# The end of a two-layer kernel: one matmul unit moved, the last gate tile by tile, the last store in halves by two queues

## The chip, the cores and the metric

The kernel runs on one core of one Trainium2 chip. The metric is the device time of one execution in microseconds (us). The profile is that of one execution; times inside it are counted from the start of its span. TensorE (PE) does the matrix products, VectorE (DVE) and ScalarE (ACT) the elementwise work, GpSimd (POOL) very little, and SyncE (SP) issues nearly all DMA transfers.

## The reference

The input `x` has 4 batches of 512 rows with 256 columns, in float32. Two layers follow each other. Each normalizes `x` over its columns, computes a mixing branch `s` and a feed-forward branch, and adds their gated product. The second layer, whose end is concerned here, cut to what matters:

```python
xn = layernorm(x)
s = causal_attention(xn)               # with its own layernorm, out-projection and residual
up_gate = einsum('bsd,hd->bsh', xn, W1)
up_lin  = einsum('bsd,hd->bsh', xn, W3)
hidden  = fwht(silu(up_gate) * up_lin) # Walsh-Hadamard transform over 1024 columns
ffn     = einsum('bsh,dh->bsd', hidden, W2)
x = x + s * silu(ffn)                  # the gate
return x
```

## The kernel before, in words

The rows of a batch form four tiles of 128 rows each (t = 0 to 3), and a tile's rows lie on the 128 partitions. The kernel walks through the four batches of the first layer and then through the four of the second, with the attention of a batch and the preparation of the next placed between the matrix products of the feed-forward part. The transform is folded into the weights `w2`. Products are done with split operands: each float32 operand is kept as a high part (rounded by ScalarE, L61) and a low part (the rest, subtracted by VectorE, L62), and three matmuls take the place of one: high by high, high by low, low by high.

`ffn_s` (L560) is the feed-forward part of one batch of the second layer. It makes the hidden values in four groups (q = 0 to 3), each of two blocks of 128 hidden columns (c = 0, 1). The down projection of tile t is a sum over all eight pairs (q, c). The inner function `down` (L577) issues it in units: one unit is one (q, c) for one tile, three matmuls of 128x256 into that tile's PSUM buffer, `f_3dn` in the profile. In the last batch each tile has a PSUM buffer of its own.

In the last batch (`last` is set) most units run between the up products, as the list `places` says. What is left is written out as a list of (q, c, t) at the end of `ffn_s`, L681 to L684. The very last group, q = 3, makes its second half of hidden values (tiles 2 and 3) in two pieces, c = 0 and c = 1 (L666 to L669): a Silu on ScalarE, a multiply on VectorE, the rounding on ScalarE, the subtraction on VectorE. The order of the matmuls is fixed as the code writes it (`line["fixed"]`, L66 to L72). On the other engines a scheduler sets the order, unless `after(...)` (L462) puts an instruction behind another; `after` fixes the order alone.

After the unit (3, 1) of a tile, which finishes its sum, `last` is called. It is `gate_tile` (L1055), which for tile t

- applies Silu to the tile's PSUM buffer on ScalarE and writes `gl` (L1058),
- multiplies `gl` by the attention branch `s` on VectorE (L1059),
- adds the product to `x` on VectorE (L1060); it reads what the multiply wrote, and waits for it on a semaphore,
- stores the tile's 128 rows of 1 KB by one DMA issued on SP (L1061).

On VectorE the scheduler had arranged the eight gate operations of the last batch in this order: multiply 0, multiply 1, add 0, add 1, multiply 2, multiply 3, add 2, add 3. The four stores stand on SP in the order of the tiles. Each DMA signals one of eight semaphores, which are taken in turn ("lanes" in this text); before a lane is used again, the issuing engine checks that its earlier transfer has landed. After the last store SP waits for all eight lanes in five wait instructions, two semaphores at most in each, and then the closing barriers of all engines follow.

ScalarE issues only two DMAs in the kernel before: loads of two tiles of `x` at the very start (L104). They run in a queue of their own, q10; SP's run in q1.

Of the kernel before, what the change touches and what calls it, by code (L numbers as in the profile page):

```python
# [17 lines left out]
ALU = mybir.AluOpType  # L18
# [3 lines left out]
P = 128  # L22
D = 256
B = 4
# [3 lines left out]
NT = S // P  # L28
# [7 lines left out]
def kernel(ctx: ExitStack, tc: tile.TileContext, a: dict, out: bass.AP):  # L36
    nc = tc.nc
# [9 lines left out]
    def t2(name, shape, dt=F32):  # L47
        return act.tile(shape, dt, tag="t2", name=name, bufs=6)
# [171 lines left out]
    def sl(i):  # L220
        return slice(i * P, (i + 1) * P)
# [240 lines left out]
    def after(ins):  # L462
        return tc.issue_after(ins.ins) if ins else nullcontext()
# [96 lines left out]
    def ffn_s(name, b, pairs, w2, beside, before, last=None):  # L560
# [16 lines left out]
        def down(q, c, hs, tiles):  # L577
            for t in tiles:
                hh, hl = (h[:, c, sl(t % 2)] for h in hs[t // 2])
                o = out_of(t)  # L580
                for n, (l, r) in enumerate(((hh, w2h), (hh, w2l), (hl, w2h))):
                    matmul(
                        o, l, r[:, 2 * q + c, :],
                        start=q + c + n == 0 and (t % 2 == 0 or last is not None),
                        stop=q == NH // 2 - 1 and c == 1 and n == 2,
                        skip_group_check=True,
                    )
# [92 lines left out]
            return behind, dns  # L680
        for q, c, t in (  # L681
            (2, 0, 2), (2, 1, 2), (2, 0, 3), (2, 1, 3), (3, 0, 0), (3, 1, 0), (3, 0, 1), (3, 1, 1),
            (3, 0, 2), (3, 0, 3), (3, 1, 2), (3, 1, 3),
        ):  # L684
            down(q, c, hidden[q], (t,))
            if (q, c) == (3, 1):
                last(t, outs[t])
# [222 lines left out]
    def run(f, *args):  # L910
        return lambda: f(*args)
# [34 lines left out]
    first = {"table": None}  # L946
# [108 lines left out]
    def gate_tile(t, o):  # L1055
        x, s = xs[B - 1][:, t, :], xns[1, B - 1][:, t, :]
        g = t2(f"gl{t}", [P, D])
        nc.scalar.activation(g, o, AF.Silu)  # L1058
        nc.vector.tensor_tensor(g, g, s, ALU.mult)  # L1059
        nc.vector.tensor_tensor(x, x, g, ALU.add)  # L1060
        nc.sync.dma_start(out[B - 1, sl(t), :], x)  # L1061

    loaded = {}

# [12 lines left out]
    for b in range(B):  # L1077
# [15 lines left out]
        if not final:  # L1093
# [3 lines left out]
            rows = run(next, norms[b + 1])  # L1097
# [14 lines left out]
            if b + 2 < B:  # L1112
                norms[b + 2] = norm(1, b + 2)
                places[3][7].append(run(next, norms[b + 2]))
            behind, dn = ffn_s(f"f1_{b}", b, pairs(b), w2_1, places, behind)
        else:
            later = [[(q, c, (2, 3)) for c in range(2)] for q in range(2)]
# [3 lines left out]
                [[later[1][0]], [later[1][1]], [], [0], [], [1], [], []],  # L1121
            ]
            ffn_s(f"f1_{b}", b, pairs(b), w2_1, places, behind, last=gate_tile)


# [66 lines left out]
```

## Time and profile before

| what | us |
|---|---|
| median of 3 runs | 359.26 (359.16 to 359.29) |
| the profiled execution | 359.27 |
| its span | 357.5 (357.49) |
| what lies around the span | 1.78 |
| busy: PE, DVE, ACT | 351.5, 287.1, 197.6 |

The profiled execution agrees with the median within 0.01 us, so its span can stand for the runs. TensorE is busy for 98% of the span, and the clock granted to it was full all the time. The time after TensorE's last matmul is short: the page puts the last matmul's end at about 353.2, and the rest of the span, some 4.3 us, is gate, stores and closing.

In the profile a line such as `351.80 0.42 DVE L1059 ...` has the start and the length in us, the engine, the source line, the operation, and `out<-in` by buffer names. An entry with `x2` merges two neighbours; its length then is from the start of the first to the end of the second. `SPq` is the instruction queue of SP, whose DMA issues are shown with the time that the issue itself takes, not the transfer.

### The profile page before, as it was taken

The numbers are of one execution on the slowest core, as the hardware profiler recorded it, in microseconds if no ns is written. First come the engines' busy times: TensorE is split into PE (matmuls) and PEld (weight loads), VectorE is DVE, ScalarE is ACT, GpSimd is POOL, SyncE is SP. The second block draws the span as 40 slices with busy tenths as digits, with TensorE's granted clock in tenths as the row PEclk, the third lists the DMA queues.
The fourth block names the chain that finished last, engine by engine and source line by source line (L and its number), as shares of the span: only waits on it lengthen the run. The fifth ranks groups of instructions, "written<-read, shape, count | busy, mean of one in ns | idle before, by whom it ended". The sixth has DMA issues, their size and how long they took to land.

```text
span 357.5 us, 6272 instructions
## 1 busy us (share of the span) xinstructions
PE 351.5 (98%) x2477; PEld 327.4 (92%) x2477; DVE 287.1 (80%) x597; ACT 197.6 (55%) x373; POOL 20.8 (6%) x22
## 2 busy tenths in 40 slices
PE   8999999999999999999999999999999999999995
PEld 6878998888988898888999999999999999999995
DVE  6899648998579938898887957989679897568645
ACT  3666156256373424674367655576555676556443
POOL 2000110300020210100110001100011000000000
PEclk9999999999999999999999999999999999999999
DMA  7935000301044416656357145562554745345401
GB/s 222 357 95 202 2 1 2 92 25 61 0 151 160 163 27 219 256 177 198 129 208 254 27 191 207 205 224 105 205 193 150 230 169 205 142 150 192 194 2 59
DMA packets 16284, 52.25 MB, mean 146 GB/s; under 512 B 1632, under 2 KB 7936, under 8 KB 16256
## 3 DMA queue, kind: packets, MB, share of 16 engines
q1 hardware_dynamic: 15968, 51.60, 41.0%
q8 instruction: 19, 0.31, 0.4%
q10 hardware_dynamic: 288, 0.26, 0.2%
q14 instruction: 9, 0.07, 0.1%
HBM read 42.40 MB, written 9.45 MB: 145 GB/s over the span
## 4 chain that ended last, share of the span: by engine, by line
PE 98%; DVE 1%; ACT 0%; issue 0%; DVEq 0%
PE f_1dn L70 6%; PE f_2dn L70 6%; PE f_1gu L70 6%; PE f_0dn L70 6%; PE f_0gu L70 6%; PE f_2gu L70 6%; PE f_3gu L70 6%; PE f_3dn L70 6%; PE sc L70 4%; PE pv L70 4%; PE o L70 3%; PE v L70 3%; PE tq L70 3%; PE warm L70 2%; PE w2ps L70 1%; PE pt L70 1%
## 5 line engine op out<-in xcount | busy, mean ns | idle before, releaser
L70 PE MATMUL f_1gu<-xt,w 128*128 128x512 f32 x96 | 24.9, 396 | 0.3 <-ACT xt L61 0.3
L70 PE MATMUL f_3gu<-xt,w 128*128 128x512 f32 x96 | 25.0, 396 | 0.0
L70 PE MATMUL f_2gu<-xt,w 128*128 128x512 f32 x96 | 24.8, 395 | 0.0
L70 PE MATMUL f_0gu<-xt,w 128*128 128x512 f32 (+1 forms) x108 | 24.4, 379 | 0.0
L70 PEld LDWEIGHTS f_0gu<-xt,w 128*128 128x128 f32 x108 | 18.5, 188 | 4.5 <-issue 1.0
L70 PEld LDWEIGHTS f_1gu<-xt,w 128*128 128x128 f32 x96 | 17.0, 188 | 3.6 <-ACT xt L61 0.5
L70 PEld LDWEIGHTS f_2gu<-xt,w 128*128 128x128 f32 x96 | 17.0, 188 | 3.0
L70 PEld LDWEIGHTS f_3gu<-xt,w 128*128 128x128 f32 x96 | 17.0, 188 | 2.9
L61 ACT CAST f_2hh<-f_2h 128x512 fp32r<-128x512 f32 x16 | 10.0, 622 | 15.3 <-DVE f_2h L527 12.2
L70 PE MATMUL f_3dn<-w2l,f_3hh 128*128 128x256 f32 x64 | 17.7, 281 | 0.0
L70 PE MATMUL f_1dn<-w2l,f_1hh 128*128 128x256 f32 x64 | 17.7, 281 | 0.0
L70 PE MATMUL f_3dn<-w2h,f_3hh 128*128 128x256 f32 x64 | 17.7, 281 | 0.0
L70 PE MATMUL f_2dn<-w2h,f_2hh 128*128 128x256 f32 x64 | 17.7, 282 | 0.0
L70 PE MATMUL f_1dn<-w2h,f_1hh 128*128 128x256 f32 x64 | 17.6, 280 | 0.0
L70 PE MATMUL f_2dn<-w2l,f_2hh 128*128 128x256 f32 x64 | 17.6, 280 | 0.0
L70 PE MATMUL f_3dn<-w2h,f_3hl 128*128 128x256 f32 x64 | 17.0, 281 | 0.0
L70 PE MATMUL f_1dn<-w2h,f_1hl 128*128 128x256 f32 x64 | 17.0, 281 | 0.0
L70 PE MATMUL f_2dn<-w2h,f_2hl 128*128 128x256 f32 x64 | 16.7, 281 | 0.0
L61 ACT CAST f_3hh<-f_3h 128x512 fp32r<-128x512 f32 (+1 forms) x17 | 10.0, 594 | 10.2 <-DVE f_3h L527 6.0
L61 ACT CAST f_1hh<-f_1h 128x512 fp32r<-128x512 f32 x16 | 9.9, 622 | 9.7 <-DVE f_1h L527 6.6
L62 DVE TENSOR_TENSOR f_2hl<-f_2h,f_2hh 128x512 fp32r<-128x512 f32 x16 | 11.0, 686 | 4.5 <-ACT f_2hh L61 4.5
L62 DVE TENSOR_TENSOR f_3hl<-f_3h,f_3hh 128x512 fp32r<-128x512 f32 (+1 forms) x17 | 11.1, 655 | 3.7 <-ACT f_3hh L61 3.6
(487 smaller groups left out, 1149.0 us busy)
## 6 DMA issues: line engine op xcount, KB each, us to landing
sw<-s SPq DMA_DIRECT2D x32, 896.0 KB, 5.3
s<-sp SPq DMA_DIRECT2D x8, 512.0 KB, 4.6
s<-sp SPq DMA_DIRECT2D x8, 384.0 KB, 2.8
w2raw<-in_w SPq DMA_DIRECT2D x4, 512.0 KB, 5.4
sraw<-in_w SPq DMA_DIRECT2D x4, 512.0 KB, 3.3
mrb<-there SPq DMA_DIRECT2D x4, 512.0 KB, 3.7
w13raw<-in_w SPq DMA_DIRECT2D x3, 512.0 KB, 6.8
x<-in_x SPq DMA_DIRECT2D x3, 512.0 KB, 3.6
```

Of the source, the lines that this page charges most:

```text
L61: h = nc.scalar.copy(hi, src)
L62: return h, engine.tensor_tensor(lo, src, hi.bitcast(F32), ALU.subtract)
L70: ins = call(*args, **kwargs)
```

## The change

Three edits, all in the end of the last batch. The last four entries of the list of units change their order: tile 2's last unit (3, 1, 2) moves ahead of tile 3's (3, 0, 3). In `gate_tile` each tile's multiply is placed behind the add of the tile before it, so that VectorE goes multiply 0, add 0, multiply 1, add 1 and so on. The store of tile 3 becomes two stores of 64 rows, the first issued on SP and the second on ScalarE; the stores of tiles 0 to 2 stay as they are.

```diff
         for q, c, t in (
             (2, 0, 2), (2, 1, 2), (2, 0, 3), (2, 1, 3), (3, 0, 0), (3, 1, 0), (3, 0, 1), (3, 1, 1),
-            (3, 0, 2), (3, 0, 3), (3, 1, 2), (3, 1, 3),
+            (3, 0, 2), (3, 1, 2), (3, 0, 3), (3, 1, 3),
         ):
...
         nc.scalar.activation(g, o, AF.Silu)
-        nc.vector.tensor_tensor(g, g, s, ALU.mult)
-        nc.vector.tensor_tensor(x, x, g, ALU.add)
-        nc.sync.dma_start(out[B - 1, sl(t), :], x)
+        with after(first.get("last")):
+            nc.vector.tensor_tensor(g, g, s, ALU.mult)
+        first["last"] = nc.vector.tensor_tensor(x, x, g, ALU.add)
+        if t + 1 < NT:
+            nc.sync.dma_start(out[B - 1, sl(t), :], x)
+            return
+
+        for queue, rows in ((nc.sync, slice(0, P // 2)), (nc.scalar, slice(P // 2, P))):
+            queue.dma_start(out[B - 1, sl(t), :][rows], x[rows])
```

In the changed program the eight lanes fall so that SP's half signals the lane that SP's third closing wait holds, and ScalarE's half the lane of the fifth; before, the only last store signals the lane of the fifth.

## The prediction

> **What bounds the kernel now.** I read the page's chain of waits first, then the timeline of its last six microseconds engine by engine, and last what the final instructions wait for. The chain says that TensorE sets the time almost everywhere; the change touches only what follows the last matmuls.
>
> ```profile
> span 357.5 us, 6272 instructions
> ...
> PE 98%; DVE 1%; ACT 0%; issue 0%; DVEq 0%
> ```
>
> The chain restricted to the end shows what that 1% of VectorE is (start, length, what):
>
> ```profile
> 351.85 0.39 ACT gl L1058
> ...
> 352.27 0.43 DVE gl L1059
> 352.69 0.67 DVE x L1060 x2
> 353.37 0.75 DVE gl L1059 x2
> 354.11 0.34 DVE x L1060
> ```
>
> From 352.27 on VectorE is never left by the chain: the end hangs on eight gate operations of VectorE in a row, not on the last matmul. The timeline of VectorE and ScalarE gives the starts:
>
> ```profile
> 351.80 0.42 DVE L1059 TENSOR_TENSOR gl<-gl,xn 128x256 f32<-128x256 f32 x1
> 352.61 0.76 DVE L1060 TENSOR_TENSOR x<-x,gl 128x256 f32<-128x256 f32 x2
> 353.33 0.78 DVE L1059 TENSOR_TENSOR gl<-gl,xn 128x256 f32<-128x256 f32 x2
> 354.03 0.76 DVE L1060 TENSOR_TENSOR x<-x,gl 128x256 f32<-128x256 f32 x2
> ...
> 352.92 0.74 ACT L1058 ACTIVATE gl<-f_3dn 128x256 f32<-128x256 f32 x2 [0.68 <-PE f_3dn L70]
> ```
>
> The order is multiply 0, 1, add 0, 1, multiply 2, 3, add 2, 3. Neighbours do not depend on each other, and so start 0.335 to 0.36 us apart although each takes 0.42: their tails overlap. The only gaps are before multiply 1 (Silu 1 ends at 352.24) and a small one before multiply 2. Silu 3 starts at 353.27, when the last matmul is done, and multiply 3 follows its end at 353.66. The last add runs from 354.37 to 354.785. Then the stores:
>
> ```profile
> 354.48 0.33 SPq L1061 DMA_DIRECT2D out<-x  x1
> 354.90 0.38 SPq L1061 DMA_DIRECT2D out<-x  x1
> ...
> SPq L1188 <- DMA out<-x: 1.1, 2, 0.7
> ```
>
> The last store could have gone at 354.81 (SP issues 0.027 after an add's end), but SP was still busy with tile 2's store and one lane check: 0.09 lost. SP's fifth final wait passes at 356.68, 1.78 after that issue; from there to the end of the span lie 0.81 us of closing barriers.
>
> **What the Trainium skill says.** "VectorE: DVE Perf Modes", section "The DRAIN you can't avoid", states of chained operations that "the semaphore costs nothing extra here". This trace disagrees for an operation that reads what the one just before it wrote. The same form, 128x256 f32, has both cases next to each other:
>
> ```profile
> 99.15 0.42 DVE L333 TENSOR_TENSOR ssum<-sraw 128x256 f32<-128x256 f32 x1
> 99.49 0.42 DVE L334 TENSOR_TENSOR ssum<-sraw 128x256 f32<-128x256 f32 x1
> 99.82 0.42 DVE L335 TENSOR_TENSOR ssum<-ssum,sraw 128x256 f32<-128x256 f32 x1
> 100.27 0.42 DVE L336 TENSOR_TENSOR ssum<-sraw,ssum 128x256 f32<-128x256 f32 x1
> ```
>
> L336 reads L335's result and starts 0.453 after it, 0.034 past its end; the others follow at 0.335. The measurement decides: a dependent neighbour costs 0.453, an independent one 0.335. "DMA: Bandwidth & Descriptors", section "Issuing engines are not separate DMA queues", says that DMAs of all issuers run on the same 16 engines and that a second issuer saves only issue time; its section "Anatomy of one DMA" puts most of a DMA's fixed cost in the write receipt. The trace fits the second: of a store's 1.73 to 1.78 us only 0.45 is packets. It shows no store from ScalarE.
>
> **The change part by part.** No instruction is added but one DMA issue on ScalarE with one lane check ahead of it; the changed program's instruction lists differ from the old ones only in this tail.
>
> *Units in another order.* The last twelve matmuls stay twelve, 0.118 us apart. Tile 2 now ends six before the end instead of three: Silu 2 starts at 352.92 - 0.35 = 352.56 (ScalarE is free from 352.24). Silu 3 and the last matmul stay where they were. What the moved unit needs last, the low part of the second half (VectorE, ends at 351.88), is read by a matmul at 352.25: 0.37 in hand, as much as the 0.35 that the first half's unit has now without a stall. Cost 0. If that cover failed, the worst is the 0.35 itself. The gain is 0 too, because VectorE isn't ready for tile 2 that early, as follows.
>
> *VectorE tile by tile.* Now each add reads the multiply just ahead of it and waits for it: the pair costs 0.453 + 0.335 instead of two times 0.335. Multiply 0 starts at 351.80 as before (it waits for the low part's subtraction ahead of it, not for Silu 0). The queue from there, each step checked against its Silu:
> - tile 0: multiply 351.80, add 352.25
> - tile 1: multiply 352.58 (Silu 1 ended at 352.24), add 353.04
> - tile 2: multiply 353.37 (Silu 2 now ends near 352.95), add 353.83
> - tile 3: multiply 354.16 (Silu 3 ended at 353.66), add 354.61, end 355.03
>
> Against 354.785 the last add ends **0.25 later**. Four dependent pairs cost 4 x 0.118 = 0.47; 0.22 is regained, because the waits on Silu 1 and Silu 2 no longer show. Behind each held add stands the next tile's multiply, so the loss passes on to the end. The stores of tiles 0 to 2 leave at 352.70, 353.49 and 354.28; they aren't last.
>
> *The last store in halves.* SP is idle by 354.7, so the 0.09 that the last store lost behind tile 2's is gone. Both halves are issued at about 355.06, 0.16 later than 354.905 now. The lane checks ahead of them wait for loads that landed long ago: 0. ScalarE has nothing behind its issue but its closing drain, which has until 356.8.
> Landing: a whole tile takes 1.73 from an idle queue (tile 2), 1.78 close behind another (tile 3). From below: the 4 KB store of row statistics at 130.83 was waited for only until 132.06, so it took 1.23 at most; with half of the 0.45 of packets 1.45. From above: the two halves share the engines and carry the same bytes, 1.73. I take 1.65 for SP's half and 1.70 for ScalarE's: nearer to the whole tile, since the bytes and the engines are the same, with a little saved on the issue. For a slow ScalarE queue there is one sign only: in the first microseconds its first packet came 1.46 after the issue, SP's 1.02; 0.44 more is the upper end.
>
> *The closing waits.* SP checks the DMA lanes in five waits, 0.065 apart when nothing holds them. Now the last store is in the fifth. In the changed program SP's half is on the lane of the third, ScalarE's on that of the fifth: after SP's half two further waits follow, 0.13, unless ScalarE's half is later by that much.
>
> Sum: 355.06 + 1.65 for SP's half + 0.13 = 356.84, against 356.68 now: **+0.15 us**, rounded. The profiled execution took 359.27 for its span of 357.49, and the median is 359.26, so I add to the median: 359.41. With the low landing (1.45) it is 356.64, or -0.04; with the late ScalarE queue 355.06 + 1.70 + 0.44 = 357.20, or +0.52.
>
> **The rivals.** 0.2% is 0.72 us, about what a measurement of this kernel can tell from no change.
> - *The dependent pair costs nothing*, as the skill's page has it. For: its statement; against: 0.453 at L336. Then multiply 3 goes at 353.69, the add ends at 354.45, the halves leave at 354.48 and the end is 356.26: -0.42, 358.84.
> - *ScalarE's queue is slow* and the kernel gets slower. That queue's last use is at 1.17 us; its first loads, like SP's, took 3.0 us to land. If its half needs 3.0 again, it lands at 358.06: +1.38, 360.64. It decides over the closing waits from a landing of 1.75 on, and makes the kernel slower by 0.2% from 2.35 on. Against: SP's first loads took just as long, so the 3.0 looks like a start, not the queue.
> - *The reordering does not do what it says*: Silu 2 is not earlier, or the halves do not spread over all engines. The first changes nothing (VectorE reaches tile 2 only at 353.37, after Silu 2's old end at 353.30); the second makes each half as long as a whole tile, 1.73, and gives 359.49, inside my range.
>
> **How the numbers follow.** The VectorE chain with ordinary landings, from -0.1 to +0.4: 0.76. ScalarE's queue late by up to half a microsecond: 0.06. Free pairs: 0.08. ScalarE's queue at over 2.35: 0.08. The remaining 0.02 is for a gain that I can't name. So faster by over 0.2%: 0.02; within: 0.90; slower: 0.08. The range, 359.15 to 359.80, holds the first two cases with the spread of the runs (0.13), and leaves out free pairs and the very late queue.
>
> **What would show it.** Right: adds at L1061 start 0.45 after their multiplies, the last ends near 355.03, both halves are issued near 355.06, the first passed wait of the last three is SP's half's. Silu 2 near 352.56 with no time gained from it. Wrong: a last add ending before 354.8; an issue to landing on ScalarE's queue well over 1.8, or under 1.45 on both; a gap in TensorE ahead of the moved unit.

## The result, and the profile after

The changed kernel takes 359.90 us (median of 17 runs, 359.79 to 360.43), the kernel before 359.26 (17 runs beside them, 358.98 to 359.46). The ratio is 1.0019, with a 95% interval of 1.0012 to 1.0026: it became slower by 0.64 us, about 0.2%. I had forecast 359.41 and a range up to 359.80. (I had also held 0.72 us for about the least that a measurement of this kernel can tell; the interval here is 0.43 to 0.93 us, which tells 0.64 from nothing.)

The page of the changed kernel, its span and its chain:

```profile
span 358.3 us, 6274 instructions
...
PE 95%; DVE 3%; DMA 1%; ACT 1%; issue 0%; DVEq 0%
```

DMA, which had no share in the chain before, has 1% now. VectorE's timeline of the end (start, length, line; multiplies at L1060, adds at L1061) shows the pairs that the change made:

```profile
351.86 0.42 DVE L1060 TENSOR_TENSOR gl<-gl,xn 128x256 f32<-128x256 f32 x1
352.31 0.42 DVE L1061 TENSOR_TENSOR x<-x,gl 128x256 f32<-128x256 f32 x1
352.65 0.42 DVE L1060 TENSOR_TENSOR gl<-gl,xn 128x256 f32<-128x256 f32 x1
...
354.24 0.42 DVE L1060 TENSOR_TENSOR gl<-gl,xn 128x256 f32<-128x256 f32 x1
354.70 0.42 DVE L1061 TENSOR_TENSOR x<-x,gl 128x256 f32<-128x256 f32 x1
```

Each add starts 0.45 us after its multiply, each multiply 0.34 after the add ahead of it. Multiply 0 starts 0.06 later than in the profile of before (351.86 against 351.80), for reasons ahead of the change. From there to the end of the last add it is 3.265 us; it was 2.988. That is 0.277 lost, and it was forecast as 0.25. ScalarE's timeline shows that Silu 2 is earlier and gains nothing, and that the issue of its half of the store is longer than the issue of a whole tile was:

```profile
352.63 0.39 ACT L1058 ACTIVATE gl<-f_3dn 128x256 f32<-128x256 f32 x1 [0.33 <-PE f_3dn L70]
353.34 0.38 ACT L1058 ACTIVATE gl<-f_3dn 128x256 f32<-128x256 f32 x1 [0.32 <-PE f_3dn L70]
355.15 0.56 ACTq L1067 DMA_DIRECT2D out<-x  x1
```

The answers on the store's line and on SP's waits (first the issue's length in ns as minimum, median, maximum; then the time from issue to landing; then what SP's closing waited for):

```profile
L1067 SPq DMA_DIRECT2D out<-x x1: 547/547/547, 355.1 to 355.1; - x1
L1067 ACTq DMA_DIRECT2D out<-x x1: 557/557/557, 355.2 to 355.2; - x1
...
DMA to landing us min/median/max: 2.0/2.1/2.3
...
SPq L1194 <- DMA out<-x: 1.5, 2, 1.3
```

Half the rows take longer to issue (0.55) than the whole tile did (0.33 to 0.38), and land 2.01 us (SP) and 2.28 us (ScalarE) after the issue; the whole last tile took 1.76. In the trace's records of single packets, SP's first packet comes 1.20 us after its issue, where whole tiles have 0.83. ScalarE's first packet comes later still, 1.50 after its issue, so that its packets come after SP's rather than among them: SP's start from 356.35 to 356.75, ScalarE's from 356.65 to 357.02.

So the loss has two parts. The last issue moved from 3.108 to 3.297 us after multiply 0, +0.19: 0.28 from VectorE, less the 0.09 that SP no longer stands in the way. From the last issue to SP's fifth closing wait it took 1.778 and takes 2.295, +0.52.

### The profile page after: what moved, and what is told of

Read it like the earlier page. It is cut to its first block, busy times and chain, and to the rows that moved or that the text cites. A ratio compares the mean times of both kernels' runs of the same rounds, so it can differ in the third digit from the quotient of the medians.

```text
span 358.3 us, 6274 instructions
## 1 busy us (share of the span) xinstructions
PE 351.4 (98%) x2477; PEld 327.2 (91%) x2477; DVE 287.3 (80%) x597; ACT 197.6 (55%) x373; POOL 20.8 (6%) x22
## 4 chain that ended last, share of the span: by engine, by line
PE 95%; DVE 3%; DMA 1%; ACT 1%; issue 0%; DVEq 0%
PE f_1dn L70 6%; PE f_2dn L70 6%; PE f_0gu L70 6%; PE f_1gu L70 6%; PE f_0dn L70 6%; PE f_2gu L70 6%; PE f_3gu L70 6%; PE f_3dn L70 5%; PE sc L70 4%; PE pv L70 4%; PE o L70 3%; PE v L70 3%; PE tq L70 3%; PE w2ps L70 1%; PE pt L70 1%; PE mps L70 1%
```

## The experiments

What comes ahead of the tail differs between profiles by up to 0.85 us (multiply 0 starts between 351.51 and 352.36), so the traces are compared by one interval: from the start of multiply 0 to the moment at which SP's fifth closing wait passes. The rest of the span behind it was 0.81 in every trace. It was 4.886 us before and 5.592 with the change: +0.706. The table gives that difference for each timed run, and the measured medians. Two further runs, with the stores cut into many pieces, were executed once each; only the lengths of their issues are used.

| run | interval, difference in us | median, and before beside it | ratio, 95% interval |
|---|---|---|---|
| the change | +0.706 | 359.90, 359.26 | 1.0019, 1.0012 to 1.0026 |
| units alone | -0.003 | 359.17, 359.19 | 0.9999, 0.9991 to 1.0007 |
| VectorE's order alone | +0.120 | 359.39, 359.19 | 1.0004, 0.9996 to 1.0012 |
| halves alone | +0.560 | 359.79, 359.19 | 1.0018, 1.0011 to 1.0025 |
| change, last store whole on SP | +0.114 | 359.32, 359.19 | 1.0003, 0.9995 to 1.0011 |
| change, last store whole on ScalarE | +0.148 | 359.38, 359.11 | 1.0004, 0.9996 to 1.0012 |
| change, both halves on SP | +1.166 | 360.32, 359.11 | 1.0032, 1.0020 to 1.0044 |
| change, tile 2's store on ScalarE | +0.704 | 359.90, 359.11 | 1.0022, 1.0014 to 1.0030 |
| change, ScalarE's half later | +0.987 | 360.23, 359.11 | 1.0030, 1.0019 to 1.0042 |
| before, tile 2's store on ScalarE | -0.074 | 359.13, 359.25 | 0.9997, 0.9988 to 1.0005 |
| change, halves by columns | +0.193 | 359.52, 359.25 | 1.0008, 1.0000 to 1.0016 |
| adds of tiles 0 and 1 on GpSimd | +0.286 | 359.58, 359.25 | 1.0008, 1.0002 to 1.0015 |
| change, 80 and 48 rows | +0.381 | 359.60, 359.19 | 1.0012, 1.0005 to 1.0018 |

### The three edits one by one

Only the units' order:

```diff
-            (3, 0, 2), (3, 0, 3), (3, 1, 2), (3, 1, 3),
+            (3, 0, 2), (3, 1, 2), (3, 0, 3), (3, 1, 3),
```

> The kernel before with the order of the units alone: (3,1,2) ahead of (3,0,3). If the unit is hidden, as predicted: Silu 2 about 0.35 us earlier, multiply 2 at most 0.05 earlier (behind add 1 by 0.335), everything from Silu 3 on unchanged, time within 0.1 us of before. If a stall of TensorE ahead of the moved unit costs something: Silu 3 later by up to 0.35 us and the time with it.

Nothing is lost and nothing gained (-0.003). Silu 2 starts at 352.63, and multiply 2 starts 0.335 behind add 1 instead of 0.387; multiply 3 still waits for Silu 3, and that for the last matmul. TensorE doesn't stall.

Only VectorE's order, all stores whole on SP:

```diff
-        nc.vector.tensor_tensor(g, g, s, ALU.mult)
-        nc.vector.tensor_tensor(x, x, g, ALU.add)
+        with after(first.get("last")):
+            nc.vector.tensor_tensor(g, g, s, ALU.mult)
+        first["last"] = nc.vector.tensor_tensor(x, x, g, ALU.add)
```

> The kernel before with VectorE's tile by tile order alone, all four stores whole on SP. Theory of the dependent pair (0.453 from a multiply to the add that reads it, 0.335 otherwise): the last add ends 0.25 to 0.28 us later, SP is idle when it comes, so the last store is issued 0.16 to 0.19 later and lands in 1.73 instead of 1.78: +0.1 to +0.2 us. If the pair costs nothing extra: the same or up to 0.4 us faster.

The last add ends 3.263 after multiply 0, the last store is issued at once and lands after 1.70: +0.120 in the trace, as the dependent pair asks. The medians say +0.20; their interval holds that and also no difference.

Only the halves:

```diff
-        nc.sync.dma_start(out[B - 1, sl(t), :], x)
+        if t + 1 < NT:
+            nc.sync.dma_start(out[B - 1, sl(t), :], x)
+            return
+
+        for queue, rows in ((nc.sync, slice(0, P // 2)), (nc.scalar, slice(P // 2, P))):
+            queue.dma_start(out[B - 1, sl(t), :][rows], x[rows])
```

> The kernel before with the last store in halves by two queues alone. VectorE as before, the last add ends near 354.8; ScalarE's half is issued near 354.81, SP's behind tile 2's store near 354.9. Theory that the pair of halves lands late (2.0 and 2.3 us after the issue as in the changed kernel): +0.3 to +0.55 us, and issues that take 0.5 us instead of 0.33 where they overlap. If only the VectorE order was the loss: 0 to +0.13.

```profile
L1066 ACTq DMA_DIRECT2D out<-x x1: 560/560/560, 355.0 to 355.0; - x1
...
L1066 SPq DMA_DIRECT2D out<-x x1: 552/552/552, 355.0 to 355.0; - x1
...
DMA to landing us min/median/max: 2.0/2.1/2.2
```

+0.560, just above the range expected and most of the whole loss, with VectorE as before. Here ScalarE's half is issued first (354.95) and SP's 0.09 behind it, and it is SP's half that lands last, 2.21 after its issue against 2.01; two closing waits then follow, 0.13. The sum of the two edits is 0.68, against 0.706 for the change: they nearly add up, although this tail is made of other parts.

The change without the halves:

> The changed kernel with its last store whole on SP again. If the halves account for what the chain on VectorE doesn't: some 0.45 to 0.55 us faster than the changed kernel, +0.1 to +0.2 against before, landing 1.73 after the issue. If the loss sits elsewhere in the change: no faster than the changed kernel, +0.6.

+0.114, with the loss of the halves gone. Its stores, all whole:

```profile
L1062 SPq DMA_DIRECT2D out<-x x4: 332/336/338, 352.9 to 355.3; - x4
...
DMA to landing us min/median/max: 1.7/1.7/1.7
```

### Why the halves land late

Three reasons were possible: two issues at the same moment hold each other up; ScalarE's queue is slow, or slow after long rest; a DMA of 64 rows is slow by itself. More than one can hold. First the queue, with the last store whole on ScalarE:

```diff
+        queue = nc.sync if t + 1 < NT else nc.scalar
+        queue.dma_start(out[B - 1, sl(t), :], x)
```

> The changed kernel with its last store whole on ScalarE's queue, SP issuing nothing at that moment. Theory of the simultaneous issue: a lone issue takes 0.33 to 0.4 us and the store lands 1.73 to 1.8 after it, time +0.1 to +0.25 against before. Theory of a slow or long unused ScalarE queue: the issue or the first packet is late, landing 2.1 to 2.3 us, time +0.5 to +0.7.

```profile
L1063 ACTq DMA_DIRECT2D out<-x x1: 354/354/354, 354.8 to 354.8; - x1
...
DMA to landing us min/median/max: 1.7/1.7/1.7
```

ScalarE's queue, last used 353 us earlier, issues in 0.354, has its first packet 0.85 after the issue, and lands in 1.72. It isn't slow. Next the change, halves and all, with tile 2's store on ScalarE, so that this queue is used 0.8 us ahead of the halves:

```diff
         if t + 1 < NT:
-            nc.sync.dma_start(out[B - 1, sl(t), :], x)
+            (nc.scalar if t == 2 else nc.sync).dma_start(out[B - 1, sl(t), :], x)
             return
```

> The changed kernel with tile 2's store moved to ScalarE's queue, which so has been used 0.8 us before the halves. Theory of a ScalarE queue that is slow for having been unused since the start: ScalarE's half is no longer late, time 0.3 us or more below the changed kernel's. Theory of the simultaneous issue: nothing changes, both issues take 0.55, time as the changed kernel's, +0.6 against before.

Nothing changes: +0.704, issues of 547 and 572 ns.

Then both halves on SP, one after the other:

```diff
-        for queue, rows in ((nc.sync, slice(0, P // 2)), (nc.scalar, slice(P // 2, P))):
+        for queue, rows in ((nc.sync, slice(0, P // 2)), (nc.sync, slice(P // 2, P))):
```

> The changed kernel with both halves of the last store issued on SP, one after the other. Theory of the simultaneous issue: the first half's issue takes about 0.3 us, its first packet comes 0.75 to 0.8 after the issue, it lands after 1.5 to 1.65; the second is issued 0.35 to 0.4 later; time +0.25 to +0.4 against before. Theory that a DMA of 64 rows is slow by itself: the first half's issue takes 0.5 or more, and it lands only after 2.0; time +0.6 or more.

```profile
L1067 SPq DMA_DIRECT2D out<-x x2: 552/570/587, 355.0 to 355.6; - x2
...
DMA to landing us min/median/max: 2.0/2.0/2.0
```

By the theory of the simultaneous issue the first half, issued alone, would take about 0.3 us; it takes 0.552, and its first packet comes 1.2 us after the issue. So the simultaneous issue isn't what makes an issue long. The same with ScalarE's half made later by a copy of the tile:

```diff
-        for queue, rows in ((nc.sync, slice(0, P // 2)), (nc.scalar, slice(P // 2, P))):
-            queue.dma_start(out[B - 1, sl(t), :][rows], x[rows])
+        rows = slice(0, P // 2), slice(P // 2, P)
+        nc.sync.dma_start(out[B - 1, sl(t), :][rows[0]], x[rows[0]])
+        late = t2("late", [P, D])
+        nc.scalar.copy(late, x)
+        nc.scalar.dma_start(out[B - 1, sl(t), :][rows[1]], late[rows[1]])
```

> The changed kernel with ScalarE's half made from a copy of the tile: ScalarE copies the tile after the last add (about 0.4 us) and stores the copy's upper 64 rows, so that its issue comes some 0.45 us after SP's. Theory of the simultaneous issue: each issue takes 0.3 to 0.35 us again, SP's half lands 1.5 to 1.65 after its issue, ScalarE's 1.5 to 1.75 after its own, so the end is 355.15 + 0.45 + 1.6 = 357.2, about 0.2 us before the changed kernel's 357.45, although its last issue is later. Theory of the slow ScalarE queue: its half still needs 2.3 after its own issue, and the time is 0.45 us above the changed kernel's.

```profile
L1067 SPq DMA_DIRECT2D out<-x x1: 553/553/553, 355.1 to 355.1; - x1
L1070 ACTq DMA_DIRECT2D out<-late x1: 541/541/541, 355.5 to 355.5; - x1
...
DMA to landing us min/median/max: 2.0/2.0/2.0
```

The issues overlap by only 0.11 now. Both still take about 0.55, and both land 2.0 after the issue, so the half is slow by itself. ScalarE's half landed after 2.28 in the change and lands after 2.02 here: the remaining 0.26 did come from the other issue at the same moment. By columns instead of rows, again two at one moment, again 64 KB each:

```diff
-        for queue, rows in ((nc.sync, slice(0, P // 2)), (nc.scalar, slice(P // 2, P))):
-            queue.dma_start(out[B - 1, sl(t), :][rows], x[rows])
+        for queue, cols in ((nc.sync, slice(0, D // 2)), (nc.scalar, slice(D // 2, D))):
+            queue.dma_start(out[B - 1, sl(t), :][:, cols], x[:, cols])
```

> The changed kernel with the last store's halves cut by columns: two stores of 128 rows of 512 bytes, on SP and on ScalarE, issued at the same moment. Theory that a store of 64 rows is slow by itself: issues of 0.33 to 0.38 us again, first packets 0.75 to 0.85 after the issue, landing 1.6 to 1.9, time +0.1 to +0.35 against before and about 0.4 below the changed kernel's. Theory that two issues at the same moment, or any half, are slow: as the changed kernel, +0.6.

```profile
L1067 SPq DMA_DIRECT2D out<-x x1: 332/332/332, 355.7 to 355.7; - x1
L1067 ACTq DMA_DIRECT2D out<-x x1: 372/372/372, 355.7 to 355.7; - x1
...
DMA to landing us min/median/max: 1.6/1.7/1.8
```

128 rows of 512 bytes are issued at the normal length and land in 1.59 and 1.77. Neither the bytes nor a second issue at the same moment makes an issue long; 64 rows do. Is it few rows in general? The stores of tiles 0 to 2 in two pieces each on SP, tile 3's whole:

```diff
+        cut = (16, 32, 48, 128)[t]
+        for rows in (slice(0, cut), slice(cut, P)):
+            if rows.start < rows.stop:
+                nc.sync.dma_start(out[B - 1, sl(t), :][rows], x[rows])
```

> The changed kernel with tiles 0 to 2 stored in two pieces of 16 and 112, 32 and 96, 48 and 80 rows, all on SP, and tile 3 whole. It measures issues by their number of rows. If every number of rows but 128 is slow: six issues of about 0.55 us. If slowness comes from few rows to an engine: 16 and 32 rows slowest, 112 near 0.33. If from 64 rows alone: all near 0.33. The time is above the changed kernel's where the queue on SP backs up into tile 3's store.

```profile
L1065 SPq DMA_DIRECT2D out<-x x7: 336/371/426, 352.8 to 355.6; - x7
```

In its trace, in order: 16 rows 336 ns, 112 rows 422, 32 rows 371, 96 rows 422, 48 rows 370, 80 rows 426, 128 rows 371 (one issue right behind another took 0.42 in the kernel before as well). None is near 550. Of what I had listed, only "64 rows alone" is left. The same with 64 rows in other places and widths, all on SP (tile 0 in 32, 64, 32 rows; tile 1 in two pieces of 64 rows by 512 bytes and one of 64 rows by 1 KB; tile 2 in 56 and 72):

> The changed kernel with all stores on SP, tile 0 in pieces of 32, 64 (rows 32 to 95) and 32 rows, tile 1 in two pieces of 64 rows by 512 bytes and one of 64 rows by 1 KB, tile 2 in 56 and 72 rows, tile 3 whole. If the count of 64 rows is the cause: the four issues of 64 rows take 0.55 to 0.6 us each, wherever they start and whatever their width, all others 0.33 to 0.43. If it is the start at partition 0 or 64, or the 64 KB in one piece: only some of the four are slow. No time is drawn from it: SP's queue backs up.

```profile
L1069 SPq DMA_DIRECT2D out<-x x9: 337/527/627, 352.4 to 357.1; - x9
```

The four issues of 64 rows take 627, 527, 598 and 594 ns: in the middle of the tile, at half the width, and at both ends. The first 32 rows take 337, 72 rows 357, 128 rows 356. The 32 and the 56 rows that stand right behind a store of 64 take 580 and 517: the issue behind it is long as well. Between 48 and 72 rows only 64 was tried with nothing slow ahead of it, so how near to 64 the slowness begins isn't known. Then a cut into 80 and 48 rows on the two queues, again at one moment:

```diff
-        for queue, rows in ((nc.sync, slice(0, P // 2)), (nc.scalar, slice(P // 2, P))):
+        for queue, rows in ((nc.sync, slice(0, 80)), (nc.scalar, slice(80, P))):
```

> The changed kernel with its last store cut into 80 rows on SP and 48 rows on ScalarE, still issued at the same moment. If 64 rows were the cause of the late landing: issues of 0.33 to 0.4 us, first packets 0.8 to 0.9 after, landing 1.6 to 1.8, time +0.1 to +0.3 against before, 0.4 to 0.5 below the changed kernel's. If cutting by rows is the cause: as the changed kernel, +0.6 to +0.75.

```profile
L1067 SPq DMA_DIRECT2D out<-x x1: 333/333/333, 354.9 to 354.9; - x1
L1067 ACTq DMA_DIRECT2D out<-x x1: 378/378/378, 354.9 to 354.9; - x1
...
DMA to landing us min/median/max: 1.8/1.9/2.0
```

The slow issue is gone with the count of 64. The loss isn't gone with it: +0.381, above the 0.1 to 0.3 that I expected. The two pieces' packets start from 355.69 to 356.39, over 0.69 us, where a whole tile's take 0.47. SP's first packet comes 0.83 after its issue, ScalarE's 1.12 after its own, although ScalarE alone had 0.85. The runs with halves at one moment agree: the second of the two issues has its first packet about 0.2 to 0.3 us later than the first has, ScalarE's in the change (1.50 against 1.20), SP's with the halves alone (1.42 against 1.21). So it isn't the queue; it is the second of two issues at one moment. What holds it up isn't shown. Every cut that was tried is behind the whole store (+0.114).

### Two attempts at something faster

Before, the last store lost 0.09 behind tile 2's on SP. With tile 2's store on ScalarE's queue and nothing else changed:

```diff
-        nc.sync.dma_start(out[B - 1, sl(t), :], x)
+        (nc.scalar if t == 2 else nc.sync).dma_start(out[B - 1, sl(t), :], x)
```

> The kernel before with tile 2's store moved to ScalarE's queue, all four stores whole. SP is free when the last add ends, so the last store is issued at once, 0.09 us earlier than before: -0.05 to -0.14 us, if two whole stores issued 0.34 apart on two queues don't hold each other up. If they do: 0 or later.

```profile
L1061 SPq DMA_DIRECT2D out<-x x3: 332/338/424, 353.0 to 354.7; - x3
L1061 ACTq DMA_DIRECT2D out<-x x1: 353/353/353, 354.4 to 354.4; - x1
```

The last issue is 3.017 after multiply 0 instead of 3.108, and the interval is 0.074 shorter. By the trace it beats both kernels; by the medians (-0.12) the gain isn't clear of the noise.

The second attempt took load off VectorE itself: the kernel before with the units in the new order, the adds of tiles 0 and 1 on GpSimd, and tile 2's store on ScalarE. I had expected 0.2 to 0.3 us less. The lines that it adds:

```diff
+        with after(first.get("last") if t > 1 else None):
+            nc.vector.tensor_tensor(g, g, s, ALU.mult)
+        engine = nc.gpsimd if t < 2 else nc.vector
+        first["last"] = engine.tensor_tensor(x, x, g, ALU.add)
+        (nc.scalar if t == 2 else nc.sync).dma_start(out[B - 1, sl(t), :], x)
```

> A version meant to be faster: the kernel before with the units in the new order, the adds of tiles 0 and 1 on GpSimd, VectorE going multiply 0, 1, 2, add 2, multiply 3, add 3, tile 2's store on ScalarE's queue, all stores whole. From the durations of the runs so far the last add ends 0.14 us earlier than before, and the last store is issued 0.24 earlier: -0.2 to -0.3 us. If GpSimd's adds slow VectorE down, or end later than tile 3's: 0 or slower.

Its timeline, GpSimd first, then VectorE:

```profile
352.53 1.87 POOL L1062 TENSOR_TENSOR x<-x,gl 128x256 f32<-128x256 f32 x2 [77.59 <-DVE gl L1060]
...
353.22 0.59 DVE L1060 TENSOR_TENSOR gl<-gl,xn 128x256 f32<-128x256 f32 x1 [0.29 <-ACT gl L1058]
353.85 0.83 DVE L1062 TENSOR_TENSOR x<-x,gl 128x256 f32<-128x256 f32 x1
354.60 0.41 DVE L1060 TENSOR_TENSOR gl<-gl,xn 128x256 f32<-128x256 f32 x1
```

While GpSimd adds, two of VectorE's operations of the same form take 0.59 and 0.83 instead of 0.42; each of them ends 0.28 after the GpSimd add that it met. (Multiply 1, which starts just ahead of GpSimd's first add, still takes 0.425.) What was taken off VectorE came back as longer operations, and the end is later by 0.286.

## Why the prediction was wrong

- **Units: right.** The moved unit costs nothing and gains nothing (-0.003), because VectorE comes to tile 2 only after Silu 2's old end.
- **VectorE tile by tile: right.** Forecast 0.25 for the last add, measured 0.277; the pair took 0.453, as at L336 of the kernel before, and the rest is that such an add takes 0.425 instead of 0.42 and the multiply behind it starts after 0.343 instead of 0.335. The rival of the free pair, built on the Trainium skill's "VectorE: DVE Perf Modes", section "The DRAIN you can't avoid" ("the semaphore costs nothing extra here"), falls here: with VectorE's order alone the last add ended 0.275 later.
- **SP free for the last store: right.** The issue moved by 0.19 (forecast 0.16).
- **The closing waits: right in size, not on the path.** The two waits behind SP's half cost 0.13 only if ScalarE's half isn't later by that; it was later by 0.27. With the halves alone they were on the path and cost 0.13. (By the prediction's own terms ScalarE's half decides from 1.65 + 0.13 = 1.78 on, not from 1.75.)
- **Landing of the halves: the step that failed.** I took 1.65 and 1.70, with 1.73 as an upper bound, because "the two halves share the engines and carry the same bytes". Measured: 2.01 and 2.28. The bound held for the packets, which started over 0.40 and 0.38, less than a whole tile's 0.47. It didn't hold for the time ahead of the first packet, which the prediction took over from a whole tile: 1.20 instead of 0.83 with 64 rows, and 1.50 for the half that was the second of two issues at one moment. In the landing, the number of rows accounts for about 0.3 (a half by itself 2.01 and 2.02, a whole tile issued by an idle SP 1.70), and the second issue for 0.26. The trace of before showed no store of 64 rows. I had bracketed 64 rows between 8 rows and 128, which is no bracket where the cost isn't monotone in the number of rows.
- **The slow queue: the wrong mechanism.** The upper end of the range came from it, and the measured time from the issue of ScalarE's half to its wait (2.295) is just under the 2.35 from which that rival makes the kernel slower by 0.2%. That nearness is chance: the queue alone lands a whole tile in 1.72, with its first packet after 0.85, so the late packets of the first loads were no property of it. Those loads were themselves two issues at one moment (SP's at 0.732, ScalarE's at 0.736), and the second had its first packet 0.44 later relative to its issue (1.46 against 1.02). So the trace of before did show such a pair. The later runs suggest that I read as a slow queue what belongs to the second issue; no run tests it at the start of the kernel. The Trainium skill's "DMA: Bandwidth & Descriptors", section "Issuing engines are not separate DMA queues", says that a second issuer saves only the time of the issue, and the runs agree: with both halves on SP the last issue came 0.60 later than in the change and the end 0.46 later. The other 0.14 that the second queue saved was lost again in the longer landing.
- **Within 0.2%: held, by luck.** The measured ratio, 1.0019, lies just inside the case to which I gave 0.90, but 0.5 of the 0.64 us come from late landings that my sum didn't hold.

The sum with the measured terms: 0.19 for the issue and 0.52 for the landing are 0.71 in the trace, and the medians say 0.64. What makes an issue of 64 rows slow inside the chip stays open; shown is only that it is the number of rows, and not the place, the row's width, the bytes, the queue, or a second issue beside it. Why the second of two issues at one moment has late packets stays open too.

## What to carry to other kernels

In this kernel an operation of VectorE on 128x256 float32 that reads what the one ahead of it wrote costs 0.12 us more than an independent neighbour (0.453 against 0.335 from start to start). So where VectorE is the end of the chain, interleave two tiles and don't finish one after the other. Be slow to split the last store: of the 1.70 us that a whole tile took from issue to landing, 0.83 lie ahead of the first packet and 0.40 behind the start of the last, and none of the five splits tried here was faster than the whole store. Look at what delays its issue instead. Before pricing a transfer of a new shape by bounds from other shapes, measure that shape once.

## What the runs showed of the hardware that was not expected

- A store of 64 rows took 0.53 to 0.63 us to issue and its first packet came 1.2 to 1.3 us after the issue, on either queue, where no other store was issued just ahead of it on the other queue; stores of 16, 32, 48, 72, 80, 96, 112 and 128 rows took 0.33 to 0.43 where no store of 64 rows stood right ahead of them.
- Of two stores issued within 0.09 us of each other on the two queues, the second had its first packet later than the first: 1.42 to 1.50 us after its issue against 1.20 with 64 rows each, 1.12 against 0.83 with 80 and 48 rows, 1.01 against 0.83 with halves by columns.
- A store of 80 rows and one of 48 on two queues started their packets over 0.69 us, a whole tile on one queue over 0.47.
- GpSimd's add of 128x256 f32 took 0.9 to 1.0 us, and VectorE's operations of that form that began while it ran took 0.59 and 0.83 instead of 0.42.
